# Per-token scalars of a four-layer graph network: products with ones against transfers through DRAM

## The chip, the cores and the metric

The kernel runs on one core of one Trainium2 chip. The metric is the device time of one execution in microseconds. A core has TensorE (PE, matmuls; its weight loads are shown apart as PEld), VectorE (DVE), ScalarE (ACT), GpSimd (POOL) and SyncE (SP), which here only issues transfers. ScalarE issues transfers too. Every engine has an instruction queue of its own; engines wait for one another by semaphores.

## The reference

128 graphs of 64 nodes, 512 features, all float32. `x` is [128, 64, 512], `adj` is [128, 64, 64], the node mask is one everywhere. Each of four layers is `x = x + f(relu(layernorm(x)), adj)`:

```python
def layer0(h, adj):            # q, k, v without bias
    agg = einsum('bij,bjd->bid', adj, k * mask)
    w   = inv_scale * mask * einsum('bid,bid->bi', q, agg)   # one scalar per token
    return softmax(w, axis=1)[:, :, None] * v                # over the 64 tokens of a graph
def layer1(h, adj):            # q, k, v with bias
    weight = adj * exp(einsum('bqd,bkd->bqk', q, k)); weight /= weight.sum(2)
    return einsum('bqk,bkd->bqd', weight, v)
def layer2(h, adj):            # 8 heads, output product with bias
    attn = softmax(scores * SCALE * (adj + adj)); return ctx @ Wo + bo
def layer3(X, A):
    Xw = X @ Wv + bv
    sj, si = Xw @ aw[:d], Xw @ aw[d:]                        # two scalars per token
    alpha = A * exp(leaky_relu(sj[:, None, :] + si[:, :, None] + ab, 0.2))
    t  = alpha / (alpha.sum(-1) + 1e-12)
    return relu(sum over k of (t^k X) @ Wk[k] + bk[k])
```

Layer 0 needs, for every token, the `w` of all 64 tokens of its graph. Layer 3 needs, for every token, the `si` of all 64 tokens of its graph.

## The kernel before

The 8192 tokens are worked in 32 blocks of 256 (TT = 2 halves of 128 partitions, so a half holds two graphs of 64). A block's 256x512 by 512x512 products are made in Strassen's manner: seven products instead of eight, with sums of the operands made on GpSimd (`sums`, L270 to L274) and sums of weights (`sums_of_weights`), which GpSimd forms while the kernel runs. `later` puts them on a list and `chore` (L100) takes some off it, each placed behind an instruction of GpSimd.

One `Product` (L278) holds two PSUM tiles, `ab` and `dc`, from four slots. `first` makes two of the seven products, `second` two, `late` three; between them `keep_ab` (L335 on ScalarE, L336 on VectorE) and `keep_dc` (L344) take partial results out of PSUM, and `store` (L358 to L362) makes the four quarters of the result on ScalarE, VectorE and GpSimd. A slot can be used again when its last reader is done. `side_by_side` runs two Products and calls the functions of a list `between` in three places: slot 0 behind the first Product's `first`, slot 1 ahead of the first `late`, slot 2 ahead of the second.

`norm` (L180) makes the layernorm of a block: statistics on VectorE (L185 to L189), `rstd` and `nmr` on GpSimd (L191, L193), `h` on ScalarE (L200), which also sends `h` to DRAM (`h_rows`, L204). SP reads it back in another arrangement (`part`, L217), and VectorE turns that into `hT` (L243), the stationary side of the products.

Layers 0 and 1 are interleaved in cycles of four steps (two blocks of layer 0, two of layer 1). Layer 2 runs over the 32 blocks, then layer 3. In layer 3, a step makes y2 and y1 side by side, then y0; two sums over neighbours stand between (`po2` ahead of y0's `late`, `po3` in the next step, L449). `layer3_end` takes po3 out by ScalarE (`tz`, L1013), adds y0 on GpSimd (L1015), and adds into `x` on VectorE (L1016). In the same step the norm of block b+2 runs and, at its end, `layer3_dots` (L915) makes that block's scalars `sij`.

A scalar of each token is put before all tokens of its graph in this way: VectorE multiplies `eye` (a 64x64 unit matrix in both halves of the partitions) with the scalars (`wd` L616, `di` L920), and TensorE multiplies by a matrix of ones for each graph:

```python
    def graph_sums(e, cols: int, name: str):
        ps = ps_sc.tile([P, cols], FP, tag="sc", name=f"sm_{name}")
        nc.tensor.matmul(ps, ones_bd, e, start=True, stop=True)
```

In layer 0, `layer0_end` reads that from PSUM (L627 to L643); in layer 3, `layer3_in` does (L934).

The tile scheduler of the language puts the instructions of each engine in one order ahead of time, by its own costs. `tc.issue_after(i)` makes it place what follows behind the instruction `i` on that order; in this way the source moves work. `tail[0]`, `kept_ab[0]`, `read[0]`, `taken` and `stored` are such instructions: the last of a layer's tail, the last `keep_ab`, the last issued read of `part` or `pT`, and the last readers in a `store`.

The seams are the steps where one layer's loop gives over to the next. At the seam to layer 2, `fetch2` loads x and `adj`, and `prepare2` adds a bias and makes the norm. At the seam to layer 3, `fetch3`, `layer3_norm` and `layer3_dots` of the first blocks are called in the last rounds of layer 2, and `biases3` (L889 to L894) loads three rows of `bk` spread over the partitions and adds them on GpSimd.

Of the kernel before, what the change touches and what calls it, by code (L numbers as in the profile page):

```python
# [13 lines left out]
P = 128  # L14
# [12 lines left out]
def kernel(ctx: ExitStack, tc: tile.TileContext, a: dict, out: bass.AP):  # L27
# [72 lines left out]
    def chore(n: int = 1):  # L100
        with tc.issue_after(behind[0].ins):
            for _ in range(min(n, len(chores))):
                w, (to, x, y) = chores.pop(0)
                nc.gpsimd.tensor_tensor(w[:, to], w[:, x], w[:, y], ALU.subtract)
# [63 lines left out]
    eye = const.tile([P, N], FP, tag="eye", name="eye")  # L168
    for g in range(2):
        h = slice(g * N, (g + 1) * N)  # L170
        nc.vector.memset(ones_bd[h, h], 1.0)
        nc.vector.tensor_copy(eye[h, :], ident[h, h])
# [4 lines left out]
    behind_norm, parted = {}, {}  # L177
    read, w2 = [None], []

    def norm(x, name: str, home):  # L180
# [13 lines left out]
        behind_norm.setdefault(0, (by_rows, summed_up))  # L194
        h = med.tile([P, TT, D], FP, tag="h", name=f"h_{name}", bufs=homes["h"])
# [60 lines left out]
    behind = [None]  # L256
# [21 lines left out]
    class Product:  # L278
# [77 lines left out]
        def store(self, y):  # L356

            nc.scalar.copy(y[:, 0, :F], self.a)  # L358
            nc.vector.tensor_tensor(self.u3, self.b, self.p1, ALU.add)
            nc.vector.tensor_tensor(y[:, 1, :F], self.d, self.u3, ALU.add)  # L360
            nc.vector.tensor_tensor(y[:, 0, F:], self.c, self.u2, ALU.add)
            nc.gpsimd.tensor_tensor(y[:, 1, F:], self.u3, self.p5, ALU.add)  # L362
# [91 lines left out]
    def graph_sums(e, cols: int, name: str):  # L454

        ps = ps_sc.tile([P, cols], FP, tag="sc", name=f"sm_{name}")
        nc.tensor.matmul(ps, ones_bd, e, start=True, stop=True)
        return ps

    def reciprocals(e, name: str):  # L460

        den = graph_sums(e.rearrange("p t i -> p (t i)"), TT * N, name)
        r = small.tile([P, TT, N], FP, tag="r", name=f"r_{name}", bufs=2)
        nc.vector.reciprocal(r.rearrange("p t i -> p (t i)"), den)
        return r
# [130 lines left out]
    def layer0(b: int, x, adjT, hs, hT, aggs, between):  # L596
# [11 lines left out]
        for t in range(TT):  # L608
            nc.vector.scalar_tensor_tensor(
                aggs[t], gv[:, 0, t, :], msc[:, b * TT + t : b * TT + t + 1], aggs[t],  # L610
                ALU.mult, ALU.mult, accum_out=w[:, t : t + 1],
            )


        wd = small.tile([P, TT, N], FP, tag="e", name=f"wd_{b}")
        tail[0] = nc.vector.tensor_tensor(  # L616
            wd,
            eye.unsqueeze(1).to_broadcast([P, TT, N]),
            w.unsqueeze(2).to_broadcast([P, TT, N]),
            ALU.mult,  # L620
        )
        return x, gv, w, wd

    def layer0_end(b: int, x, gv, w, wd):
        wrow = graph_sums(wd.rearrange("p t i -> p (t i)"), TT * N, f"w_{b}")
        mn = small.tile([P, TT], FP, tag="mx0", name=f"mn0_{b}")
        nc.vector.tensor_reduce(  # L627
            mn, wrow.rearrange("p (t i) -> p t i", t=TT), AX.X, ALU.min
        )
        nc.vector.tensor_tensor(w, w, mn, ALU.subtract)  # L630
        tot = small.tile([P, TT], FP, tag="tot", name=f"tot_{b}")
        for t in range(TT):
            nc.scalar.activation(
                wd[:, t, :], wrow[:, t * N : (t + 1) * N], AF.Exp, bias=mn[:, t : t + 1],
# [272 lines left out]
    def layer3_dots(b: int, x, adjT, hs):  # L907
# [4 lines left out]
        for s in range(2):  # L912
            for t in range(TT):
                hu = med.tile([P, D], FP, tag="agg", name=f"hu_{b}_{s}_{t}", bufs=2)
                nc.vector.scalar_tensor_tensor(  # L915
                    hu, hs[t], 1.0, us[s], ALU.mult, ALU.mult,
                    accum_out=sij[:, s, t : t + 1],
                )
        di = small.tile([P, TT, N], FP, tag="e", name=f"di_{b}")
        nc.vector.tensor_tensor(  # L920
            di,
            eye.unsqueeze(1).to_broadcast([P, TT, N]),
            sij[:, 1, :].unsqueeze(2).to_broadcast([P, TT, N]),
            ALU.mult,
        )
# [4 lines left out]
    def layer3_in(b: int, x, adjT, hs, e, sj, made: dict):  # L930


        pi = graph_sums(e.rearrange("p t i -> p (t i)"), TT * N, f"i_{b}")
        nc.vector.tensor_tensor(  # L934
            e,
            pi.rearrange("p (t i) -> p t i", t=TT),
# [188 lines left out]
    for i, (layer, b) in enumerate(steps):  # L1125
        if i == n_steps - 4:
            fetch2(0)
        if i == n_steps - 3:
            fetch2(1)
        if i == n_steps - 1:  # L1130
            fetch2(2)
        between = [[], [lambda: chore(3 if i < 4 else 1)], []]
# [20 lines left out]
        elif i + 2 == n_steps:  # L1153
            between[0].append(lambda: prepare2(0))
        else:
            between[0].append(lambda: prepare2(1))
        if layer == 0:
            softmax = layer0(b, *loaded[b], *normed[i], aggs.pop(b, None), between)
            begun = [(0, lambda b=b, softmax=softmax: layer0_end(b, *softmax))]
# [23 lines left out]
    def layer3_step(b: int, ahead: bool = True):  # L1183
# [8 lines left out]
        def begin():  # L1192
# [3 lines left out]
            if b + 2 < n_blk and ahead:  # L1196
                with tc.issue_after(kept_ab[0].ins):
# [16 lines left out]
        if b + 2 < n_blk:  # L1214
            with tc.issue_after(kept.ins):
                if ahead:
                    normed3 = layer3_dots(b + 2, *normed3)
                    fetch3(b + 3)
                else:
                    fetch3(b + 2)  # L1220
# [17 lines left out]
    for b in range(n_blk):  # L1238
        x = loaded2[b][0]
        first_in = lambda: layer3_in(0, *normed3, made_in) if b == n_blk - 2 else None  # L1240
        if b + 1 < n_blk:
            pTs = []
# [5 lines left out]
            def ahead():  # L1248
                with ExitStack() as placed:
                    for i in (pTs[1], kept_c[0], read[0]):  # L1250
                        placed.enter_context(tc.issue_after(i.ins))
                    prepare2(b + 3)
                with tc.issue_after(read[0].ins):
# [5 lines left out]
        else:  # L1259
            pTs = layer2_turned(b, es)  # L1260
# [6 lines left out]
        if b == n_blk - 2:  # L1267
            w3[0] = fetched("L3_Wk0", 4, nc.sync)
            later(w3[0])
            bias3 = biases3()  # L1270
        if b + 1 < n_blk:
            coming = values(b + 1, ops)
            next(coming)
        else:
# [15 lines left out]
        if b + 1 < n_blk:  # L1290
            with tc.issue_after(of_o.kept.ins):
                layer2_divided(b + 1, es)
        chore(2 if b == n_blk - 2 else 0)
# [3 lines left out]
        if n_blk - 3 <= b < n_blk - 1:  # L1297
            fetch3(b - n_blk + 3)
            normed3 = layer3_norm(b - n_blk + 3)
            with tc.issue_after(of_o.taken.ins):  # L1300
                normed3 = layer3_dots(b - n_blk + 3, *normed3)
        elif b == n_blk - 1:
            with tc.issue_after(of_o.taken.ins):
                normed3 = layer3_dots(2, *normed3)
            fetch3(3)
# [69 lines left out]
```

## Time and profile before

| | |
|---|---|
| time, median of 3 runs | 2525.49 us (2525.25 to 2526.71) |
| profiled execution | 2527.11 us, of which the span of instructions is 2524.5 us |
| mean granted clock of TensorE | 0.996 |
| TensorE matmul, busy | 2487.0 us, 19488 instructions |
| VectorE, busy | 1822.0 us, 4590 instructions |
| GpSimd, busy | 1324.1 us, 1710 instructions |
| ScalarE, busy | 857.1 us, 2106 instructions |
| transfers | 295.50 MB, 117 GB/s on average |

The profile comes from one execution. Its rows name an engine, a line of the kernel, an operation, the tiles that it writes and reads, and times. A wait is put down to the instruction or transfer that released it last. The clock is the share of TensorE's full speed that was granted in a stretch.

### The profile page before, as it was taken

Reading aid. Unit: us, or ns where it says so; the run is one execution under the profiler, and the core shown is the slowest. Engines: PE = TensorE matmul, PEld = TensorE weight load, DVE = VectorE, ACT = ScalarE, POOL = GpSimd, SP = SyncE. Lnnn points to the kernel's source line nnn. Section 1 sums busy time; section 2 is a strip of 40 time slices with the busy share of each in tenths; the row PEclk is TensorE's granted clock in tenths of the full one; section 3 lists DMA queues with packets and bytes.
Section 4 is the critical chain, followed back from the end, with each engine's and each line's share of the span. In section 5 each row is a group of like instructions: output and inputs, shape, how many; then the busy total and the mean of one; then the engine's idle time right before and its main releaser. Section 6 shows DMA issues by size and latency. Waiting matters only on the chain.

```text
span 2524.5 us, 52284 instructions
## 1 busy us (share of the span) xinstructions
PE 2487.0 (99%) x19488; PEld 2124.1 (84%) x19488; DVE 1822.0 (72%) x4590; ACT 857.1 (34%) x2106; POOL 1324.1 (52%) x1710
## 2 busy tenths in 40 slices
PE   9899999999999999999999999999989999999999
PEld 5788888888888888999999999999867777777776
DVE  5577777777777786667667667667568777777775
ACT  3333433333334332333333333333223333333332
POOL 2444343444433445666656556556465555555554
PEclk9999999999999999999999999999999999999999
DMA  7344343333343354443343343344433333333320
GB/s 180 94 127 124 111 127 114 119 107 116 113 126 112 122 156 138 128 133 108 122 132 115 123 131 115 122 136 134 139 112 104 104 103 107 105 106 106 103 77 34
DMA packets 305190, 295.50 MB, mean 117 GB/s; under 512 B 56870, under 2 KB 211494, under 8 KB 304936
## 3 DMA queue, kind: packets, MB, share of 16 engines
q1 hardware_dynamic: 258856, 208.26, 29.2%
q10 hardware_dynamic: 46080, 83.91, 9.1%
q8 instruction: 153, 2.51, 0.4%
q14 instruction: 101, 0.83, 0.1%
HBM read 158.91 MB, written 133.18 MB: 116 GB/s over the span
## 4 chain that ended last, share of the span: by engine, by line
PE 57%; DVE 2%; DMA 1%; POOL 1%; issue 1%; SPq 0%; ACT 0%; POOLq 0%; ACTq 0%; DVEq 0%
PE ab_y L306 13%; PE dc_y L306 9%; PE ab_v L306 4%; PE ab_q L299 4%; PE ab_k L299 4%; PE ab_o L306 4%; PE dc_q L299 3%; PE dc_k L299 3%; PE dc_v L306 3%; PE dc_o L306 3%; PE po L449 2%; PE pc L825 1%; PE s L750 1%; DVE hu L915 1%; DMA x<-x 0%
## 5 line engine op out<-in xcount | busy, mean ns | idle before, releaser
L200 ACT ACTIVATE h<-x,nmr,rstd 128x512 f32<-128x512 f32 x256 | 194.8, 806 | 207.6 <-POOL nmr L193 202.1
L270 POOL TENSOR_TENSOR S<-hT 128x256 f32<-128x256 f32 x128 | 97.8, 764 | 243.9 <-DVE hT L243 231.1
L306 PE MATMUL ab_y<-L_Wk,hT 128*128 128x256 f32 x768 | 204.9, 389 | 7.9 <-DVE u_y L336 6.7
L306 PE MATMUL ab_v<-L_Wv,hT 128*128 128x256 f32 x768 | 201.0, 384 | 3.7 <-DVE u_v L336 3.0
L306 PEld LDWEIGHTS ab_y<-L_Wk,hT 128*128 128x128 f32 x768 | 138.7, 190 | 74.9 <-DVE u_y L336 30.7
L191 POOL TENSOR_TENSOR rstd<-ve,neghalf 128x2 f32<-128x2 f32 x128 | 90.5, 707 | 209.2 <-DVE mv L189 190.7
L306 PE MATMUL dc_v<-L_Wv,S 128*128 128x256 f32 x768 | 198.0, 380 | 0.7 <-ACT p_v L344 0.7
L306 PE MATMUL ab_y<-L_Wk,S 128*128 128x256 f32 x768 | 198.0, 380 | 0.0
L306 PE MATMUL ab_v<-L_Wv,S 128*128 128x256 f32 x768 | 197.1, 379 | 0.0
L306 PE MATMUL dc_y<-L_Wk,S 128*128 128x256 f32 x768 | 193.5, 380 | 0.1
L243 DVE STREAM_TRANSPOSE hT<-part 128x512 f32<-128x512 f32 x252 | 174.4, 698 | 8.6 <-DMA part<-h_rows 5.9
L306 PEld LDWEIGHTS dc_y<-L_Wk,S 128*128 128x128 f32 x768 | 146.0, 191 | 21.3 <-issue 0.8
L306 PEld LDWEIGHTS ab_y<-L_Wk,S 128*128 128x128 f32 x768 | 146.5, 191 | 20.1
L185 DVE BATCH_NORM_STATS2 stats<-x 128x6 f32<-128x512 f32 x256 | 162.8, 677 | 0.0
L306 PEld LDWEIGHTS ab_v<-L_Wv,S 128*128 128x128 f32 x768 | 145.9, 190 | 19.8
L306 PEld LDWEIGHTS dc_v<-L_Wv,S 128*128 128x128 f32 x768 | 143.8, 191 | 20.0 <-ACT p_v L344 0.9
L306 PEld LDWEIGHTS ab_v<-L_Wv,hT 128*128 128x128 f32 x768 | 138.2, 190 | 21.9 <-DVE u_v L336 4.0
L915 DVE SCALAR_TENSOR_TENSOR hu<-h,us 128x512 f32<-128x512 f32 x128 | 139.4, 1139 | 1.9 <-POOL bs L894 1.4
L1015 POOL TENSOR_TENSOR tz<-tz,y 128x512 f32<-128x512 f32 x62 | 90.4, 1458 | 95.4 <-ACT tz L1013 95.3
L336 DVE TENSOR_TENSOR u_v<-ab_v,p_v 128x256 f32<-128x256 f32 x96 | 40.4, 421 | 126.4 <-ACT p_v L335 125.9
L1016 DVE SCALAR_TENSOR_TENSOR x<-tz,x 128x512 f32<-128x512 f32 x62 | 42.9, 692 | 112.3 <-POOL tz L1015 112.3
L272 POOL TENSOR_TENSOR S<-hT,S 128x256 f32<-128x256 f32 x128 | 113.0, 883 | 0.0
(257 smaller groups left out, 6181.7 us busy)
## 6 DMA issues: line engine op xcount, KB each, us to landing
x<-x SPq DMA_DIRECT2D x128, 512.0 KB, 3.8
h_rows<-h ACTq DMA_DIRECT2D x252, 256.0 KB, 2.1
part<-h_rows SPq DMA_DIRECT2D x504, 128.0 KB, 2.8
x<-in_x_dram SPq DMA_DIRECT2D x32, 512.0 KB, 3.7
e_rows<-et ACTq DMA_DIRECT2D x64, 256.0 KB, 3.0
pT<-e_rows SPq DMA_DIRECT2D x128, 128.0 KB, 3.1
out_dram<-x SPq DMA_DIRECT2D x31, 512.0 KB, 2.8
adjT<-in_adjT_dram SPq DMA_DIRECT2D x64, 64.0 KB, 2.2
```

What stands on the lines that cost most here:

```text
L185: nc.vector.bn_stats(stats[:, t, :], x[:, t, :])
L191: nc.gpsimd.tensor_tensor(rstd, ve, neghalf, ALU.pow)
L200: nc.scalar.activation(hs[t], x[:, t, :], AF.Relu, bias=nmr[:, t : t + 1], scale=rstd[:, t : t + 1])
L243: nc.vector.transpose(hT[:, :, t * P : (t + 1) * P].rearrange("p k (g q) -> p g k q", q=Q), part[:, t * 4 : (t + 1) * 4].rearrange("p g (k ...
L270: nc.gpsimd.tensor_tensor(S1, A21, A22, ALU.add)
L272: nc.gpsimd.tensor_tensor(S4, A12, S2, ALU.subtract)
L299: nc.tensor.matmul(dst[:, m * P : (m + 1) * P], w[:, place, k, m * P : (m + 1) * P], left[:, k, :], start=key not in self.begun, stop=last ...
L306: nc.tensor.matmul(dst, left[:, k, :], w[:, place, k, :], start=key not in self.begun, stop=last and k == 1, skip_group_check=True,)
L449: nc.tensor.matmul(ps[t][half[g ^ t]], e[half[g], t, :], us[t][half[g]], start=True, stop=True)
L915: nc.vector.scalar_tensor_tensor(hu, hs[t], 1.0, us[s], ALU.mult, ALU.mult, accum_out=sij[:, s, t : t + 1],)
L1015: nc.gpsimd.tensor_tensor(tz[t], tz[t], y0[:, t, :], ALU.add)
L1016: nc.vector.scalar_tensor_tensor(x[:, t, :], tz[t], 0.0, x[:, t, :], ALU.max, ALU.add)
```

## The change

Five things are changed together.

1. `spread` takes the place of `graph_sums` and of the products with `eye`, in layer 0 (for `w`) and layer 3 (for `si`): SP writes the 256 scalars of a block as rows into DRAM, and reads them back twice, once for each 64 partitions, repeated over the partitions. The result lies in SBUF instead of PSUM, and `layer3_in` and `layer0_end` work in its place.
2. `layer0_end` is called in slot 1 of the next step instead of slot 0, and `tail` is the last of layer 0's dots.
3. `chore`'s weight sums are placed also behind the last `store` on GpSimd and the last `nmr`.
4. At the seam from layer 1 to 2, `fetch2` comes earlier and the norm of block 0 and 1 is placed behind `tail`. At the seam from layer 2 to 3, the loads, norms and dots of blocks 0 and 1 come earlier and are placed by hand, the last block's turning of `e` comes earlier, and the loads of the biases come behind the reads of `pT`.
5. In layer 3, the norm of block b+2 is placed behind `spread_out` (the last read of the spread) as well as behind `kept_ab`, and the load of block b+3 behind the reads of `part`.

```diff
+    spread_out = [None]
+
+    def spread(of_tokens, name: str):
+        row = tc.dram_tile([TT, P], FP, name=f"{name}_row")
+        nc.sync.dma_start(row.rearrange("t p -> p t"), of_tokens)
+        to = small.tile([P, TT, N], FP, tag="e", name=name)
+        by_graph = row.rearrange("(o t) (g i) -> g o t i", o=1, g=2)
+        for g in range(2):
+            spread_out[0] = nc.sync.dma_start(
+                to[half[g]], by_graph[g].to_broadcast([N, TT, N])
+            )
+        return to
...
-    def chore(n: int = 1):
-        with tc.issue_after(behind[0].ins):
+    def chore(n: int = 1, also=()):
+        with ExitStack() as placed:
+            for i in (behind[0], *also):
+                placed.enter_context(tc.issue_after(i.ins))
...
+        normalised[0] = by_rows
...
+            stored[0] = nc.gpsimd.tensor_tensor(y[:, 1, F:], self.u3, self.p5, ALU.add)
...
-        wd = small.tile([P, TT, N], FP, tag="e", name=f"wd_{b}")
-        tail[0] = nc.vector.tensor_tensor(
-            wd, eye..., w..., ALU.mult)
-        return x, gv, w, wd
+        return x, gv, w, spread(w, f"w_of_{b}")
...
-        wrow = graph_sums(wd.rearrange("p t i -> p (t i)"), TT * N, f"w_{b}")
...
+        nc.vector.tensor_reduce(mn, wd, AX.X, ALU.min)
...
-        di = small.tile([P, TT, N], FP, tag="e", name=f"di_{b}")
-        nc.vector.tensor_tensor(
-            di, eye..., sij[:, 1, :]..., ALU.mult)
+        di = spread(sij[:, 1, :], f"si_of_{b}")
...
-        pi = graph_sums(e.rearrange("p t i -> p (t i)"), TT * N, f"i_{b}")
...
-        if i == n_steps - 4:
-            fetch2(0)
-        if i == n_steps - 3:
-            fetch2(1)
-        if i == n_steps - 1:
-            fetch2(2)
-        between = [[], [lambda: chore(3 if i < 4 else 1)], []]
+        if i >= n_steps - 6 and i % 2 == 0:
+            fetch2((i + 6 - n_steps) // 2)
+        between = [[], [
+            lambda: chore(3 if i < 4 else 1, (stored[0], normalised[0]) if i else ())
+        ], []]
...
-            begun = [(0, lambda b=b, softmax=softmax: layer0_end(b, *softmax))]
+            begun = [(1, lambda b=b, softmax=softmax: layer0_end(b, *softmax))]
...
             if b + 2 < n_blk and ahead:
-                with tc.issue_after(kept_ab[0].ins):
+                with tc.issue_after(kept_ab[0].ins), tc.issue_after(spread_out[0].ins):
                     normed3 = layer3_norm(b + 2)
...
                 if ahead:
                     normed3 = layer3_dots(b + 2, *normed3)
-                    fetch3(b + 3)
+                    with tc.issue_after(read[0].ins):
+                        fetch3(b + 3)
...
-            pTs = layer2_turned(b, es)
...
-            bias3 = biases3()
...
+            if b == n_blk - 2:
+                normed3 = layer3_dots(
+                    1, *normed3_1[0], (of_qk[b + 1][1].taken, kept_ab[0])
+                )
...
+        if b == n_blk - 2:
+            with tc.issue_after(read[0].ins):
+                fetch3(2)
+                fetch3(3)
+            with tc.issue_after(of_o.taken.ins):
+                pTs = layer2_turned(b + 1, es)
+            with tc.issue_after(read[0].ins):
+                bias3 = biases3()
...
-        if n_blk - 3 <= b < n_blk - 1:
-            fetch3(b - n_blk + 3)
-            normed3 = layer3_norm(b - n_blk + 3)
+        if b == n_blk - 3:
+            fetch3(0)
+            fetch3(1)
+            with tc.issue_after(read[0].ins):
+                normed3 = layer3_norm(0)
             with tc.issue_after(of_o.taken.ins):
-                normed3 = layer3_dots(b - n_blk + 3, *normed3)
+                normed3 = layer3_dots(0, *normed3)
```

## The prediction

> **What bounds the kernel now.** I read the page's busy times first, then TensorE's waits and three stretches, then the order of one step of layer 3.
>
> ```profile
> PE 2487.0 (99%) x19488; PEld 2124.1 (84%) x19488; DVE 1822.0 (72%) x4590; ACT 857.1 (34%) x2106; POOL 1324.1 (52%) x1710
> ...
> PE 57%; DVE 2%; DMA 1%; POOL 1%; issue 1%; SPq 0%; ACT 0%; POOLq 0%; ACTq 0%; DVEq 0%
> ```
>
> TensorE is busy for 2487.0 of 2524.5 us, so at most 37.5 us of idle time can be had by moving work, plus whatever products are removed. VectorE has 28% to spare as an average, which says little about one step.
>
> ```profile
> PE ab_y L306 <- DVE u_y L336: 6.7, 2, 6.5
> ...
> PE sm_w L457 <- DVE wd L616: 4.5, 2, 3.9
> PE ab_g L306 <- DVE u_g L336: 3.9, 2, 3.2
> ...
> PE pc L825 <- DMA pT<-e_rows: 2.8, 2, 1.7
> ```
>
> These are TensorE's waits (total, times, longest). The 6.5 and the 2.8 lie at the seam from layer 2 to 3, the 3.9 and the 3.2 in the first 100 us. By stretches:
>
> ```profile
> 300.00:900.00 600.00, 599.76 (x4227) 514.26 (x4226) 446.44 (x1206) 231.90 (x600) 242.19 (x365) 1.00 0.39 118
> 960.00:1740.00 780.00, 780.00 (x8510) 719.02 (x8507) 540.98 (x1265) 255.41 (x661) 474.49 (x604) 1.00 0.41 124
> 1900.00:2470.00 570.00, 570.00 (x2999) 451.83 (x2998) 448.68 (x1141) 183.50 (x383) 332.70 (x381) 1.00 0.32 101
> ```
>
> The columns after the length are busy TensorE, weight loads, VectorE, ScalarE, GpSimd, then the granted clock. In all three steady stretches TensorE never waits at full clock. A removed product there is time saved, and a new wait there is time lost, undiluted.
>
> **Products removed.** TensorE at the sum of one block of layer 3:
>
> ```profile
> 2110.51 0.38 PE L457 MATMUL sm_i<-di,ones_bd 128*128 128x128 f32 x2
> 2110.73 1.03 PE L306 MATMUL ab_y<-L_Wk,hT 128*128 128x256 f32 x4
> ```
>
> From start to start it takes 0.22 us; in layer 0 (718.98 to 719.20) the same. 64 of them: 14.1 us at most. The 64 VectorE products with `eye` (0.28 us each, 18 us) go too, but VectorE isn't what ends the steps above.
>
> **What stands in their place.** A row write of 256 four-byte elements, then two reads that wait for it, all on SP: 192 issues more (0.33 to 0.46 us each, so about 1.2 us a block on a queue that is mostly idle). No transfer like it is in the trace. The nearest rows:
>
> ```profile
> adjT<-in_adjT_dram SPq DMA_DIRECT2D x64, 64.0 KB, 2.2
> ...
> c_row<-c SPq DMA_DIRECT2D x4, 0.5 KB, 6.3
> ```
>
> The reads should land like `adjT` (2.2). The write lies between 2.2 and 6.3; `c_row` also moves four-byte elements, but stood beside 256 KB broadcasts at the start, so I take about 2.5. With two issues the chain is about 5.5 us, at most 9.3. The Trainium skill ("DMA: Bandwidth & Descriptors", Anatomy of one DMA) gives a DMA a fixed cost of about 2.0 us, spent mostly on the receipt of the last byte, which speaks against two dependent transfers in place of a product; by it the chain would be an estimated 4.9 us, and the 6.3 of `c_row` says that it can be much more.
>
> **Layer 3, 28 steady steps of 20.9 us.** The decisive edit is not the transfer but what is tied to it: `layer3_norm(b+2)` is now issued behind `spread_out`, so its BN statistics (VectorE L185) come after the four `hu` products instead of before `y<-po`. One step before:
>
> ```profile
> 2116.47 1.28 DVE L185 BATCH_NORM_STATS2 stats<-x 128x6 f32<-128x512 f32 x2
> ...
> 2123.06 0.90 DVE L915 SCALAR_TENSOR_TENSOR hu<-h,us 128x512 f32<-128x512 f32 x1
> ...
> 2132.74 0.69 DVE L1016 SCALAR_TENSOR_TENSOR x<-tz,x 128x512 f32<-128x512 f32 x1 [1.16 <-POOL tz L1015]
> 2133.35 0.42 DVE L359 TENSOR_TENSOR u_y<-ab_y,p_y 128x256 f32<-128x256 f32 x1
> ```
>
> ScalarE's `h` of the same block stood at 2119.34, where ScalarE had 1.9 us to spare; in the new order it stands, with its two DMA issues, directly ahead of the last `p_y` and of `tz` (L1013). So `tz` queues behind `h`, `h` behind GpSimd's `rstd`, that behind VectorE's statistics, those behind `hu`. I count from the first half of po2 (2117.6 on this step's clock):
>
> - `y<-po` 2.27, then two `hT` and four `y0` operations 2.53 (2120.53 to 2123.06): 4.8.
> - four `hu` 4.24 (to 2127.30): 9.05. `sj` 0.13, statistics 1.2: 10.4. Aggregates, `ve`, `mv` and one `u_y`: 11.2.
> - `rstd` and `nmr` (2118.32 to 2119.30) 0.98: 12.2. Two `h` and their issues (2119.34 to 2121.21) 1.9: 14.1. `p_y`: 14.45, where `tz` starts. Before it started at 2128.82, that is 11.2: 3.2 us later.
> - `tz` to GpSimd 0.77, GpSimd 1.26, `x` 0.65, `u_y` of y2 (L359, L360 in the changed file) 0.42: 17.55. TensorE wants that PSUM slot for y0 at 2134.22 less the 0.22 removed, 16.4: it waits 1.1. The second `tz` on GpSimd ends at 18.3, `x` at 18.95, the two `y` that free the other slot at 19.65, and y0's second half starts at about 19.85 where it was at 18.35 (2135.95).
>
> So a step grows by about 1.5 with the removed product already counted. Each hand-over is uncertain by some 0.1, and GpSimd and VectorE will overlap a little differently; I take 1.4 x 28 = +39. From below: the chain hides wholly and only 0.22 a step is saved, -6. From above: the write takes 6.3, `si_of` lands at about 9.05 + 0.4 + 6.3 + 0.5 + 2.2 = 18.45, and its addition, which VectorE has ahead of both `x`, moves `y` from 19.65 to 21.35: 1.7 x 28 = 48 more. At my 5.5 it lands at 14.6, before `x` at 16.5, free. On SP the two reads wait for the write, and behind them stand the reads of `part`, which wait for `h` at 14 anyway: no loss.
>
> That `fetch3(b+3)` moves behind the reads of `part` costs nothing: x is asked for at about 19 and used in the next step at 31.
>
> **Layers 0 and 1, 15 cycles of four steps.** Their spreads have a whole slot to land, and what is queued behind them on SP (loads of x and `part`) is asked for more than a step ahead: hidden at 5.5 us, and up to the +15 below if not. Each cycle loses two sums (0.44). With `layer0_end` in slot 1, its reduction, exponentials and `x` additions (1.34 to 1.84 us on VectorE) now stand ahead of the `gT` stores, and the norm of the pair that follows stands on ScalarE ahead of `p_v`. By hand `p_v` comes within 0.3 us of its need, and the `gT` slot 0.2 to 0.7 late. A cycle nets -0.44 to +1.0; I take +0.2: +3 (from -6 to +15).
>
> **Start.** The 3.9 at `sm_w` came from the dots waiting for GpSimd's y (L362) behind weight sums; `chore` now stands behind `stored`. The 3.2 at `ab_g` followed from the same queue. Both went with about 2 us of slowed products. Up to -9; but layer 0's first spreads meet the weight loads that made `c_row` 6.3, and VectorE's `mn0` stands in order: up to +5. I take -4.
>
> **Seam 1 to 2.** Earlier loads of layer 2: TensorE idles 3.2 us in 940 to 960. -2 (0 to -3).
>
> **Seam 2 to 3.** TensorE idles 2.8, 6.5 and 1.5 here.
>
> ```profile
> 1800.00:1830.00 30.00, 27.24 (x291) 25.36 (x290) 20.34 (x46) 7.69 (x22) 14.58 (x17) 0.94 0.60 157
> 1830.00:1850.00 20.00, 13.49 (x53) 11.05 (x53) 11.35 (x24) 1.76 (x5) 17.59 (x19) 0.83 0.34 109
> ```
>
> The 6.5 was `u_y` L336 behind `hu` L915 behind GpSimd's `bs` L894; `dots(1)` is now earlier and the biases are behind pT's reads. The three groups after it took 4.88 us where 2.6 is usual, so the clock adds 2.3. Up to -13; the new waits (si_of(0) ahead of `qk`'s VectorE work, another load in the way) take 0.3 to 5 back. -10.
>
> **Sum:** 39 + 3 - 4 - 2 - 10 = +26 on the profiled execution, 2527.1 (span 2524.5 and 2.6 around it): 2553; the median lies 1.6 lower, so 2551. A measurement of this kernel tells about 0.2%, 5 us, from no change.
>
> **Rivals.**
> A. Layer 3 keeps TensorE as its bound (faster). The place is the same chain; it decides at a `tz` less than about 2.3 us late instead of 3.2, since the other terms give 13 and 13 over 28 steps is 0.46 a step, 0.9 less than I read. If it hides wholly: -6 + 3 - 4 - 2 - 10 = -19, 2506; with layers 0 and 1 and the seams at their best, 2490. For it: ScalarE is 34% busy and the norm has a whole step to spare. Against: engines here keep their written order, and the order puts `h` ahead of `tz`.
> B. The row write is slow (near 6.3) also in layer 3. Then 2551 + 48 at the worst, near 2570 to 2600. For it: only one row of four-byte writes, and it says 6.3. Against: DMA share is 0.32 there and 0.59 at the start.
> C. The gains and the chain cancel (layer 3 at +0.3 to +0.6 a step): 2520 to 2530.
>
> **Chances.** Forecast (2535 to 2570) 0.52; A 0.28; B 0.13; C 0.07. Leaving out A's lowest and B's highest, the range is 2499 to 2578. Faster by over 0.2%: A and a part of C, 0.31; within: 0.04; slower: 0.65.
>
> **What would show it.** In the changed profile, layer 3's stretch should hold new TensorE waits on `ab_y` and `dc_y` released by VectorE's `u_y` L360 and `y`, about 1 us a step, and a period near 22.3; `tz` on ScalarE directly behind `h`. `si_of` should land within 6 us of its write's issue. The wait of 6.5 and the 3.9 should be gone. I am wrong if the period is 20.7, if `si_of` is what VectorE waits for, or if layers 0 and 1 grow by more than 15 us.

## The result, and the profile after

The changed kernel takes 3007.61 us (median of 4 runs, 2999.23 to 3009.02) against 2525.53 us: 1.190 times as long, interval 1.188 to 1.192. The forecast was slower, at 2551 us, with 2578 as the upper end: the sign was right and the size was off by a factor of nineteen. The profiled execution took 3008.35 us, its span is 3006.6 us, the mean granted clock 0.936. Of the 12 runs of l3_best below, two fell in a slower state (2576.39 and 5172.51 us), and its time is the median of the other ten.

The page of the changed kernel, its busy times and its chain:

```profile
PE 2618.2 (87%) x19360; PEld 2206.1 (73%) x19360; DVE 1786.6 (59%) x4524; ACT 855.8 (28%) x2106; POOL 1318.8 (44%) x1710
...
PE 54%; DMA 20%; DVE 16%; issue 3%; POOL 3%; ACT 2%; SPq 1%; ACTq 0%; DVEq 0%; POOLq 0%
```

Transfers are now 20% of the chain that ends last, where they were 1%. TensorE has 128 matmuls fewer and is busy 131 us *longer*; its idle time went from 37.5 to 388.4 us. Both add up to the 482 us of the span. Who is waited for, first on TensorE, then on VectorE:

```profile
PE ab_y L307 <- DVE u_y L360: 210.2, 30, 8.7
PE ab_v L307 <- DVE u_v L337: 74.4, 18, 6.7
```

```profile
DVE si_of L918 <- DMA si_of<-si_of_row: 317.8, 31, 12.0
DVE mn L619 <- DMA w_of<-w_of_row: 212.5, 32, 10.1
```

TensorE waits for VectorE's `u_y`, which does no more than before; VectorE waits 31 times for `si_of` and 32 times for `w_of`, each about 10 and 7 us. The transfers, in the list of DMA issues (the last number is the median time from issue to landing):

```profile
x<-x SPq DMA_DIRECT2D x128, 512.0 KB, 4.4
...
w_of<-w_of_row SPq DMA_DIRECT2D x64, 32.0 KB, 4.2
si_of<-si_of_row SPq DMA_DIRECT2D x64, 32.0 KB, 3.7
...
w_of_row<-w SPq DMA_DIRECT2D x32, 1.0 KB, 8.2
...
si_of_row<-sij SPq DMA_DIRECT2D x32, 1.0 KB, 9.0
```

The write of 1 KB takes about twice as long as the transfers of 512 KB (`x<-x`, 4.4 us). One step of layer 3, on SP, VectorE and TensorE:

```profile
2616.39 0.36 SPq L460 DMA_DIRECT2D si_of_row<-sij  x1
2626.22 1.23 SPq L464 DMA_DIRECT2D si_of<-si_of_row  x2
```

```profile
2629.81 0.29 DVE L918 TENSOR_TENSOR si_of<-si_of,sj 128x128 f32<-128x128 f32 x1 [11.04 <-DMA si_of<-si_of_row]
...
2630.95 0.42 DVE L360 TENSOR_TENSOR u_y<-ab_y,p_y 128x256 f32<-128x256 f32 x1
```

```profile
2600.08 2.07 PE L307 MATMUL ab_y<-L_Wk,hT 128*128 128x256 f32 x4 [7.15 <-DVE u_y L360]
...
2607.08 1.13 PE L307 MATMUL ab_y<-L_Wk,hT 128*128 128x256 f32 x4
...
2631.42 0.80 PE L307 MATMUL ab_y<-L_Wk,hT 128*128 128x256 f32 x1 [7.83 <-DVE u_y L360]
```

The write is issued at 2616.39, the reads can start only at 2626.22, `si_of` is added at 2629.81: 13.4 us. `u_y` stands behind that addition on VectorE, and TensorE's y0 behind `u_y`. In the kernel before, the same addition of block b+1 stood behind both `x` and behind y2's first stores, where it held up neither:

```profile
2134.54 0.28 DVE L934 TENSOR_TENSOR di<-sm_i,sj 128x128 f32<-128x128 f32 x1
```

So the change also brought the reader forward on VectorE. A step takes 31.3 us (2600.08 to 2631.42) where it took 20.9. After such a wait four matmuls take 2.07 us instead of 1.13: the granted clock is 0.50 from 2600.1 to 2604.0. Over layers 0 and 1 it is 0.93 on average and over layer 3 0.90, where it was 1.00 and 0.99; that is where most of the 131 us of busy time come from. The Trainium skill ("TensorE: Matmul & The Clock Gate", Part 1) says that an idle window of about 3.4 us puts TensorE back to half its clock; the 0.50 after a wait of 7.15 us agrees. A shorter wait can bring it here too: in l3_best_norm_late, below, four matmuls took 2.07 us after a wait of 1.86 us, at a granted clock of 0.50, while in pairs four took 1.13 us after a wait of 2.67 us. In the runs below whose waits in a step stay at or under 3.6 us (prod_norm_late, l3_best_norm_late, quick, pairs) busy time rises by 12 to 26 us instead of 131.

Where the time went, by stretches cut at TensorE's first product of layer 2, its last q product of layer 2, and its first product of layer 3 (profiled executions, us; "seam" is from the second cut to the third; the versions below are explained with their experiments):

| kernel | layers 0, 1 | layer 2 | seam | layer 3 to the end |
|---|---|---|---|---|
| before | 961.0 | 846.7 | 24.3 | 692.5 |
| changed | 1155.1 | 845.4 | 35.0 | 971.1 |
| pairs | 1007.0 | 845.6 | 28.0 | 790.4 |
| quick | 995.0 | 845.6 | 24.9 | 764.7 |
| late_in | 1167.5 | 845.4 | 31.5 | 802.2 |
| l3_best_norm_late | 961.2 | 845.7 | 29.7 | 769.4 |
| l3_best | 961.9 | 845.6 | 29.8 | 680.4 |
| prod | 965.5 | 845.8 | 22.3 | 683.4 |
| prod_slot1 | 959.6 | 845.9 | 22.3 | 683.5 |
| prod_seam | 957.3 | 845.9 | 22.7 | 683.8 |
| l0_quick | 994.4 | 845.8 | 22.4 | 683.4 |
| final | 955.8 | 845.6 | 20.9 | 678.1 |

### The profile page after: what moved, and what is told of

Same layout as the page of the kernel before. It is cut to its first block, busy times and chain, and to the rows that moved or that the text cites. A ratio compares the mean times of both kernels' runs of the same rounds, so it can differ in the third digit from the quotient of the medians.

```text
span 3006.6 us, 52286 instructions
## 1 busy us (share of the span) xinstructions
PE 2618.2 (87%) x19360; PEld 2206.1 (73%) x19360; DVE 1786.6 (59%) x4524; ACT 855.8 (28%) x2106; POOL 1318.8 (44%) x1710
## 4 chain that ended last, share of the span: by engine, by line
PE 54%; DMA 20%; DVE 16%; issue 3%; POOL 3%; ACT 2%; SPq 1%; ACTq 0%; DVEq 0%; POOLq 0%
PE ab_v L307 9%; DMA si_of_row<-sij 8%; PE dc_v L307 6%; DVE hu L906 4%; PE ab_y L307 4%; PE ab_q L300 4%; PE ab_k L300 4%; DMA w_of<-w_of_row 4%; PE ab_o L307 4%; DMA si_of<-si_of_row 4%; DMA w_of_row<-w 3%; PE dc_q L300 3%; PE dc_k L300 3%; PE dc_o L307 3%; PE dc_y L307 2%
## 5 line engine op out<-in xcount | busy, mean ns | idle before, releaser
L307 PE MATMUL ab_y<-L_Wk,hT 128*128 128x256 f32 x768 | 234.9, 434 | 220.8 <-DVE u_y L360 210.2
L307 PEld LDWEIGHTS ab_y<-L_Wk,hT 128*128 128x128 f32 x768 | 153.2, 211 | 303.7 <-DVE u_y L360 222.2
L307 PE MATMUL ab_v<-L_Wv,hT 128*128 128x256 f32 x768 | 217.8, 409 | 85.3 <-DVE u_v L337 74.4
L307 PE MATMUL ab_y<-L_Wk,S 128*128 128x256 f32 x768 | 223.6, 419 | 0.0
L307 PE MATMUL ab_v<-L_Wv,S 128*128 128x256 f32 x768 | 209.5, 398 | 0.0
L918 DVE TENSOR_TENSOR si_of<-si_of,sj 128x128 f32<-128x128 f32 x32 | 10.0, 314 | 317.8 <-DMA si_of<-si_of_row 317.8
L307 PEld LDWEIGHTS ab_y<-L_Wk,S 128*128 128x128 f32 x768 | 163.9, 213 | 27.1
L307 PEld LDWEIGHTS dc_y<-L_Wk,S 128*128 128x128 f32 x768 | 156.9, 205 | 33.2 <-ACT p_y L345 5.4
L336 ACT COPY p_y<-ab_y 128x256 f32<-128x256 f32 x96 | 35.7, 372 | 385.2 <-PE ab_y L307 384.7
L363 POOL TENSOR_TENSOR y<-u_y,p_y 128x256 f32<-128x256 f32 x64 | 57.2, 894 | 188.1 <-DVE u_y L360 188.1
L619 DVE TENSOR_REDUCE mn<-w_of 128x2 f32<-128x128 f32 x32 | 9.2, 286 | 212.5 <-DMA w_of<-w_of_row 212.5
```

Of the source, the lines that this page charges most:

```text
L307: nc.tensor.matmul(dst, left[:, k, :], w[:, place, k, :], start=key not in self.begun, stop=last and k == 1, skip_group_check=True,)
L336: kept_p[0] = nc.scalar.copy(self.p1, self.a)
L363: stored[0] = nc.gpsimd.tensor_tensor(y[:, 1, F:], self.u3, self.p5, ALU.add)
L619: nc.vector.tensor_reduce(mn, wd, AX.X, ALU.min)
L918: nc.vector.tensor_tensor(e, e, sj.unsqueeze(2).to_broadcast([P, TT, N]), ALU.add,)
```

## The experiments

**Theory.** What costs is the length of the spread, most of it the write, because VectorE's order puts its reader ahead of work that TensorE waits for. Rivals: the order of the norm (the prediction's own mechanism), the number of transfers on SP, the other edits.

**Why the write is slow: probe.** Writes that nobody reads, in seven forms, added to the kernel before.

```diff
+        nc.sync.dma_start(to, of)    # form = b % 7, behind layer3_dots
```

> The kernel before, with one more transfer a block of layer 3 that nobody reads: the write of the scalars to DRAM in seven forms in turn (block number modulo 7), on SP behind the same dots. fa4: the change's own form, 256 elements of four bytes to one run of 1 KB. fb8: the same bytes as 128 pieces of 8. fc64 and fd512: 256 elements of four bytes, each 64 or 512 bytes from the next. fe_half: 128 elements of four bytes. ff_quarter: 64 elements. fg_wide: 128 pieces of 256 bytes. Theory (each small piece costs the queue by itself): fa4, fc64 and fd512 all land in 8 to 9 us as in the changed kernel, fb8 and fe_half in about 5, ff_quarter in 3 to 4, fg_wide near 5 or less. Rival (neighbouring elements fall into the same short stretch of DRAM and their writes wait for one another): fc64 and fd512 land in about 2.5 us, fa4 in 8 to 9. Second rival (it is the traffic around it): all seven land alike, in 2 to 4 us here. The time stays at 2525 to 2530 in all cases, since nobody waits.

```profile
fg_wide<-h SPq DMA_DIRECT2D x4, 32.0 KB, 1.8
...
fa<-sij SPq DMA_DIRECT2D x5, 1.0 KB, 9.5
fb<-sij SPq DMA_DIRECT2D x5, 1.0 KB, 3.6
fc<-sij SPq DMA_DIRECT2D x5, 1.0 KB, 1.7
fd<-sij SPq DMA_DIRECT2D x5, 1.0 KB, 1.7
fe_half<-sij SPq DMA_DIRECT2D x4, 0.5 KB, 8.6
ff_quarter<-sij SPq DMA_DIRECT2D x4, 0.2 KB, 6.6
```

The theory of a price for each piece fell: the same 256 pieces of four bytes land in 1.7 us when they lie 64 bytes apart, and in 9.5 side by side. That rules out the traffic around as well. The run took 2531.0 us, 1 us more than expected.

**How near is too near: probe2 and probe3.**

```diff
+            to = tc.dram_tile([TT, P, pitch], FP, ...)[:, :, 0]   # pitch 2, 4, 8: px, py, pz
+            to = tc.dram_tile([16, P], FP, ...)[:, :8]            # qf: runs of 8, 512 bytes apart
+            to = tc.dram_tile([8, 16], FP, ...).rearrange("a e -> e a")   # qg: turned
```

> The kernel before, again with transfers in layer 3 that nobody uses, block number modulo 8. px, py, pz: the 256 four-byte scalars written with 8, 16 and 32 bytes from one to the next (contiguous they landed in 9.5 us, 64 bytes apart in 1.7). pw: 32 of them, contiguous. ra, rb, rc: what reads them back over 64 partitions, from a contiguous row (the change's read), from pairs of 8 bytes side by side, and from a row spaced by 64 bytes. Theory (writes into the same 64 bytes of DRAM wait for one another): the time falls with the number that share them, px about 5, py about 3, pz about 2, pw about 5. Rival (they wait only where they touch the next one): px, py and pz all about 1.7. Reads: ra 2.5 to 4, rb no longer than ra, rc far longer (10 us or more), since it moves 16384 pieces of four bytes.

> The kernel before with unread writes of four-byte scalars in layer 3, one column, block number modulo 7. qa: 32 contiguous, qb: 64 contiguous, qd: 128 contiguous (8.6 before). qc: 16 pairs of 8 bytes, contiguous. qe: 128 spaced by 8 bytes. qf: 16 runs of 8 neighbours, the runs 512 bytes apart, so that pieces of the same run come from neighbouring partitions. qg: 128 contiguous in DRAM but turned, so that neighbours in DRAM come from partitions 8 apart and neighbouring partitions lie 64 bytes apart. Theory A (pieces that follow one another on one DMA engine wait where they touch the same 64 bytes; neighbouring partitions go to the same engine): qf about as long as qd, qg about 2 us. Theory B (pieces of different engines collide in the same 64 bytes): qf 4 us or less, qg about as long as qd.

```profile
px<-sij SPq DMA_DIRECT2D x4, 1.0 KB, 4.3
py<-sij SPq DMA_DIRECT2D x4, 1.0 KB, 2.7
pz<-sij SPq DMA_DIRECT2D x4, 1.0 KB, 1.9
...
pw<-sij SPq DMA_DIRECT2D x4, 0.1 KB, 1.3
```

```profile
qa<-sij SPq DMA_DIRECT2D x5, 0.1 KB, 4.1
...
qd<-sij SPq DMA_DIRECT2D x5, 0.5 KB, 7.1
...
qf<-sij SPq DMA_DIRECT2D x4, 0.5 KB, 1.8
qg<-sij SPq DMA_DIRECT2D x4, 0.5 KB, 7.3
```

At 4, 8, 16, 32 and 64 bytes from piece to piece the write takes 9.5, 4.3, 2.7, 1.9 and 1.7 us. So it is closeness in DRAM that costs, and pieces need not touch for it. Runs of eight touching pieces from neighbouring partitions are quick (`qf` 1.8) if the runs lie 512 bytes apart. 128 touching pieces are slow also when neighbours in DRAM come from partitions 8 apart (`qg` 7.3), so it is not that neighbouring partitions touch: theory A is out. Theory B fits both, but it is not the only reading, since the time also rises with the number of touching pieces: `pw`, from 16 partitions, takes only 1.3, well under what was expected, 32 pieces take 4.1 (`qa`), 128 take 7.1 (`qd`). A run of eight pieces from far partitions was not written, so whether the far partitions or the long run is what counts stays open, as does the unit in DRAM. A slow write can also hold up what follows it: `rowb` of probe2, in the form of `fb` and issued 0.5 us behind a row in the change's form, landed in 8.5 us, where `fb` took 3.6.

Of the reads, the change's own took 3.4, from pairs 3.0, from a row spaced by 64 bytes 6.7 each for four reads instead of two, less than the 10 that were expected. The runs took 2526.1 and 2529.2 us.

**The write alone: pairs, and later quick.** The changed kernel with a different row in DRAM.

```diff
-        row = tc.dram_tile([TT, P], FP, name=f"{name}_row")
-        nc.sync.dma_start(row.rearrange("t p -> p t"), of_tokens)
+        row = tc.dram_tile([P, TT], FP, ...)       # pairs: 8 bytes a partition
+        row = tc.dram_tile([16, P], FP, ...)[:, :8 * TT]   # quick: 16 runs of 64 bytes, 512 apart
```

> The changed kernel with one edit: the row in DRAM holds the two scalars of a partition side by side (128 pieces of 8 bytes, 3.6 us in the probe instead of 9.5), and each partition reads 512 bytes in one piece. Nothing is moved. Theory (the length of the spread is what VectorE waits for, step by step): some 5.5 us less a block in layer 3 and about as much in layer 0, so 2660 to 2740. Rival (the number of transfers on SP costs as well): over 2800.

> The changed kernel with the quick row in both layers and nothing else altered: the write lands in about 2 us where it took 9, the spread in about 6.5 where it took 13. Theory (the write is most of it, the rest is the late norm and the remaining wait in both layers): layer 2 starts at 990 to 1000, layer 3 takes 750 to 780, total 2600 to 2630. If the order alone costs what l3_best_norm_late showed and the quick spread is hidden: 2570 to 2590. Rival (the transfers' number): 2660 or more, as with pairs.

2672.8 and 2632.1 us. The writes landed in 3.0 to 3.5 us with pairs and 1.8 to 2.3 with quick, and 335 and 376 of the 482 us went, with no instruction moved. TensorE's busy time fell from 2618.2 to 2512.8 and 2503.4, with the shorter waits. Quick missed its expected range by 2 us.

**The reader moved: late_in.** The spread as it was, its reader in layer 3 behind y0's stores.

```diff
-            if b + 1 < n_blk:
+            if b + 1 < n_blk and not b:
                 layer3_in(b + 1, *coming, made_in)
...
+        if b and b + 1 < n_blk:
+            with tc.issue_after(kept.ins):
+                layer3_in(b + 1, *coming, made_in)
```

> The changed kernel with the spread in both layers as it is, but layer3_in of block b+1 behind y0's last store in step b instead of ahead of both x additions: VectorE comes to si_of about 16 us later in the step. Theory (the chain of some 13 us only costs because VectorE's order has its reader in front of work that TensorE waits for): layer 3 falls from 971 to 690 to 735 us, the total to 2725 to 2770, layers 0 and 1 unchanged. Rival (the transfers themselves slow others, by the queue on SP or the DMA engines): layer 3 stays above 850 us.

2848.4 us; layer 3 fell from 971.1 to 802.2, so the reader's place is most of what layer 3 lost. That lies between the two expectations (690 to 735, and above 850), and layers 0 and 1, which this does not touch, took 12 us more. What was undercounted is above all the late norm, as the next runs show. With it and no wait for a spread layer 3 takes 769.4 (l3_best_norm_late); what the other 33 us are was not traced.

**The norm: prod_norm_late, prod, and l3_best_norm_late.** Products back in both layers; then the norm in its old place; and the same pair with the spread.

```diff
-        di = spread(sij[:, 1, :], f"si_of_{b}")
+        di = beside_eye(sij[:, 1, :], f"di_{b}")    # both kernels; w in layer 0 likewise
...
+        pi = graph_sums(e, f"i_{b}")
...
-                with tc.issue_after(kept_ab[0].ins), tc.issue_after(spread_out[0].ins):
+                with tc.issue_after(kept_ab[0].ins):
                     normed3 = layer3_norm(b + 2)
...
-                    with tc.issue_after(read[0].ins):
-                        fetch3(b + 3)
+                    fetch3(b + 3)
```

> The changed kernel with the products with ones back in both layers (layer0_end again in slot 0), but with all other edits, and the norm of layer 3 as late in VectorE's order as in the changed kernel. Theory (the spread's length is what costs): nearly all of the 482 us go, but the late norm keeps the chain from hu through the statistics, rstd, h and tz, so layer 3 runs at 22.3 us a step: 2535 to 2555. Rival (the order of the norm costs nothing by itself): 2508 to 2516. Rival (the other edits, weight sums and seams, cost a large part): over 2600.

> The same, with the norm of layer 3 back in its old place (its two conditions and the one on fetch3 taken off). What is left of the change is the order of the weight sums and both seams. Theory: layer 3 at 20.9 us a step, the start and the seams better by what the prediction gave them, -16: 2508 to 2516. Rival (the edits at the seams give nothing): 2523 to 2530.

2595.48 us (1.0284, 1.0268 to 1.0299) and 2515.99 us (0.9967, 0.9956 to 0.9979). The late norm costs 79.5 us over 28 steps, 2.8 a step. That is more than was expected of the late norm (2555 at most) and less than of a large cost of the other edits (over 2600). Part of it there is the products' own: TensorE waits 40.9 us for a slot of PSUM that `tz` still reads. So the pair was repeated with the spread, whose reader comes a whole step later and never waits:

```diff
-                layer3_in(b + 1, *coming, made_in)
+            with tc.issue_after(kept_ab[0].ins):
+                layer3_in(b, *held3.pop(b), made_in)    # held3[b]: what layer3_dots(b) left
...
-        first_in = lambda: layer3_in(0, *normed3, made_in) if b == n_blk - 2 else None
+        first_in = lambda: held3.update({0: normed3}) if b == n_blk - 2 else None   # l3_best
```

> The version with products (2516) with the spread in layer 3 alone, in the change's slow form, but layer3_in of block b one step later, in step b itself behind y1's keep_ab: the transfer has more than 20 us, and VectorE's order is that of the kernel before. Theory (the transfer costs nothing where its reader comes later than it lands, and a product is worth 0.22 us): 2516 less 31 times 0.22, 2507 to 2511. Rival (192 small transfers disturb TensorE's supply in other ways): 2520 or more.

> l3_placed with block 0 of layer 3 treated like the others: its layer3_in no longer stands in layer 2's last rounds, where VectorE waited 9.4 us for its spread ahead of qk, but in step 0. Spread in layer 3 in the change's slow form, products in layer 0, norm in its old place. Theory: the 9.4 go, and the 0.22 of each block of layer 3 is left as a gain over the version with products (2516): 2508 to 2513. Rival (the transfers cost elsewhere): 2516 or more.

> l3_best with the norm of layer 3 as late as in the change (both its conditions, and fetch3 behind the reads). No reader waits for a spread, and no product takes a slot of PSUM: this is the prediction's chain from hu to tz alone. As predicted, 1.4 to 1.5 us a step: 39 to 42 us slower than l3_best. If the 2.8 us a step that the late norm cost in the version with products hold here too: 75 to 80. If the chain has slack: 0 to 10.

l3_placed: 2524.97 us (0.9999, 0.9989 to 1.0009), a miss. Layer 3 is at 681.2 us there, but one wait at the seam is left:

```profile
PE ab_v L307 <- DVE qk L376: 9.4, 1, 9.4
```

It is block 0's spread, whose reader stands in layer 2's last rounds ahead of `qk`, as in the change (9.5 there). l3_best takes it away: 2519.66 (0.9977, 0.9967 to 0.9986), above what was expected, since the seam still takes 29.8 us where prod has 22.3; the quick row of best_quick brings it to 21.7 (1803.8 to 1825.5), so there too it is the write's length. In l3_best layer 3 takes 680.4 us, 3 less than with products (prod 683.4): the slow transfers by themselves cost next to nothing in it. With the late norm 2609.59 (two runs): 90 us more than l3_best, 3.2 a step, above all three expectations. One step of it, on VectorE, and GpSimd's store beside the second `x`:

```profile
2211.58 0.69 DVE L1020 SCALAR_TENSOR_TENSOR x<-tz,x 128x512 f32<-128x512 f32 x1 [4.43 <-POOL tz L1019]
2212.19 0.42 DVE L360 TENSOR_TENSOR u_y<-ab_y,p_y 128x256 f32<-128x256 f32 x1
2213.43 1.20 DVE L1020 SCALAR_TENSOR_TENSOR x<-tz,x 128x512 f32<-128x512 f32 x1 [0.82 <-POOL tz L1019]
...
2218.51 2.28 DVE L981 SCALAR_TENSOR_TENSOR y<-po,r,y 128x512 f32<-128x512 f32 x3 [0.49 <-PE po L450]
```

```profile
2213.36 0.73 POOL L363 TENSOR_TENSOR y<-u_y,p_y 128x256 f32<-128x256 f32 x1
```

The next `y<-po` starts at 2218.51, and the `hT` that follows comes 23.5 us after that of the step before (2197.36 to 2220.83). Quick, the changed kernel with nothing but the quick row, takes 764.7 in layer 3, no more than these 769.4. So the two mechanisms account for layer 3: with the write quick, what is left of its loss is no more than the late norm costs.

**Layer 0: l0_placed, prod_slot1, l0_quick.** The spread in layer 0 alone, with `layer0_end` a step later; its place in slot 1 without a spread; its place with a quick spread.

```diff
-            begun = [(0, lambda b=b, softmax=softmax: layer0_end(b, *softmax))]
+            begun = [(1, lambda b=b, softmax=softmax: layer0_end(b, *softmax))]   # prod_slot1, l0_quick
+            after_next.append(lambda b=b, softmax=softmax: layer0_end(b, *softmax))   # l0_placed
```

> The version with products (2516) with the spread in layer 0 alone, in the change's slow form, and layer0_end not in the next step but in the one after it, behind the tail of the step between. Theory: the wait at w_of goes, and 31 products less: 2507 to 2513. Rival (the x additions and exponentials so placed delay the stores of the step they fall into): 2520 to 2560. If the spread's wait stays on VectorE: over 2600.

> The version with products (2516) with layer0_end in slot 1 of the next step, as in the change. Theory (the place alone costs little, the spread's length costs the rest): 2516 to 2522. Rival (the x additions ahead of the gT stores are what costs): 2530 to 2600.

> The version with products in layer 3, and in layer 0 the change's spread and its layer0_end in slot 1, but with a row in DRAM made of 16 runs of 64 bytes, the runs 512 bytes apart, each from 8 neighbouring partitions (such runs of 32 bytes landed in 1.8 us in the probe), so the spread takes about 6 us in place of 13. Theory: the first product of layer 2 starts at 960 to 1000 us where it started at 1155 in the changed kernel, total 2515 to 2555. Rival (it is the number of transfers, or the order): over 2580.

2552.46 us (1.0098, 1.008 to 1.0117; in the rival's range), 2513.52 us (0.9952, 0.9934 to 0.997) and 2547.8 us. The place in slot 1 costs nothing, it rather gains. A spread of some 6 us there still costs 35 us up to layer 2 (994.4 against 959.6), so layer 0's reader comes sooner than the transfer's end even then (VectorE waits 40.6 us for `w_of` in l0_quick). With the reader a step later VectorE waits only 4.1 us for `w_of` in all, but TensorE waits for `u_v` and `u_g` (18.0 and 12.1 us in l0_placed); what holds these up I did not trace. Neither version with a spread in layer 0 alone paid; the quick row with the reader a step later was not run.

**What is left: l3_best_seam, prod_seam, best_quick, final.** l3_best and prod with the seam from layer 1 to 2 as before; the first of these with the quick row of above (best_quick); that with `layer0_end` in slot 1 (final).

```diff
-        if i >= n_steps - 6 and i % 2 == 0:
-            fetch2((i + 6 - n_steps) // 2)
+        if i == n_steps - 4:
+            fetch2(0)
+        ...
```

> The same, with the seam from layer 1 to 2 as before (fetch2 later, the norms of blocks 0 and 1 not behind the tail). Theory (that edit gains nothing: TensorE idles 5.0 us in 900 to 1000 us with it and 3.2 without): 2 to 5 us faster than the one above. Rival (it gains the 2 us that the prediction gave it): 2 us slower.

> The version with products (2516) with the seam from layer 1 to 2 as in the kernel before: what is left of the change is the order of the weight sums and the seam to layer 3. Theory (the first seam's edit loses some 3 us, as l3_best and l3_best_seam showed): 2511 to 2515. Rival: 2516 or more.

> l3_best_seam (2517) with the quick row for layer 3's spread. Theory (its 6 us of idle TensorE at the seam to layer 3 are waits for the slow write and what queues behind it on SP): 2509 to 2514. Rival (the transfers' place, not their length, disturbs that seam): 2515 to 2518.

> best_quick (2505.6) with layer0_end in slot 1 of the next step, which gained 2.5 us in the version with products. If the gains add: 2502 to 2504. If not: 2505 to 2508.

2516.95 us (0.9963, 0.9951 to 0.9974), 2512.65 (0.9948, 0.9936 to 0.9961), 2505.56 (0.9921, 0.9907 to 0.9934; better than the 2509 to 2514 expected) and 2502.03 us (0.9910, 0.9893 to 0.9926). The last beats both kernels: products in layer 0, a quick spread read a step later in layer 3, the norm where it was, the weight sums and the seam to layer 3 as the change has them. Its page:

```profile
PE 2474.1 (99%) x19424; PEld 2113.3 (85%) x19424; DVE 1812.5 (72%) x4558; ACT 861.4 (34%) x2106; POOL 1309.3 (52%) x1710
```

## Why the prediction was right or wrong

- **The reading of the profile held.** In the steady stretches a removed product is time saved undiluted: best_quick is 7.1 us faster than prod_seam, 31 or 32 products at 0.22 as read off 2110.51 and 2110.73. And new waits there were time lost undiluted.
- **The step that failed is the price of the row write.** The term that was mis-sized is the chain of about 5.5 us for a spread, which took 13.4. For the write I had one row of its kind, `c_row` at 6.3 us, and 2.2 for reads; I took 2.5, on the ground that `c_row` stood beside large loads. That ground was never tested, and the probe shows it false: the same form takes 9.5 us in layer 3, where the traffic is light (DMA share 0.32 before). Even the upper end was too low: `si_of` was to land at worst at 18.45 us after po2, and was added 22.6 us after the start of `y<-po` (2607.18 to 2629.81). "The decisive edit is not the transfer but what is tied to it" is so the wrong way round: the quick row alone takes 206 us out of layer 3 and 160 out of layers 0 and 1, and the late norm costs 77 to 90. Rival B had the right mechanism, at 13%, with too small a price. That the sign was right is not luck, since the late norm alone makes the kernel slower; but it says little, as most of the loss came from elsewhere.
- **The place of the reader was half seen.** I wrote that the addition stands ahead of both `x` on VectorE and counted 1.7 us a step for a late landing. Measured, a step grew by 10.4 us. With the quick row layer 3 falls by 206 us of its 279, with the reader moved (late_in) by 169; the two overlap, since each takes away the same wait.
- **The clock was left out.** I counted it at the seam (2.3 us) and not in a steady step. But waits like that of 7.15 us come in nearly every step (210.2 us in 30), and the clock falls after them; TensorE's busy time grew by 131 us, about half of it in layer 3 and half in layers 0 and 1.
- **The late norm: right mechanism, half the size.** The chain was right to 0.1 us as far as `u_y`: in l3_best_norm_late `tz` starts 14.46 us after `y<-po` (counted 14.45), `u_y` ends after 17.56 (17.55). But I set the start 0.6 us after po2's first matmul, where VectorE starts 1.1 after it, and the second `x` took 1.20 us beside GpSimd's store, not 0.69. Most steps take 23.5 us, 2.6 more than before, not 1.4; the average is 3.2 us more than l3_best, since some steps take over 25 us, as where the clock falls after the wait of 1.86 us. Whether `fetch3` behind the reads costs nothing, as I wrote, no run shows by itself: each run that put the norm back took that condition off with it. In l3_best_norm_late, which has it, VectorE waits for no load of x in layer 3.
- **Layers 0 and 1** were the worst term in proportion: +3, at most +15, measured +194 up to layer 2's first product, start and first seam included. I wrote that the spreads have a whole slot to land. VectorE waited 6.6 us a block for them (212.5 over 32), and with the quick row of some 6 us still 40.2 us in all. Behind the spreads on SP stand the reads of `part`, for which VectorE waits 29.0 us in the changed kernel and 5.9 before, most of it here (26.0). The cost of the order, which I counted by hand, was the smaller matter: prod_slot1 has it and takes 2513.52 us, prod 2515.99 (medians of different sets).
- **The start** was right in size: prod_seam, which has only the order of the weight sums there, reaches layer 2 at 957.3 instead of 961.0, -3.7 where -4 was taken (one profile each). Of its mechanism half came true: the 3.9 at `sm_w` is gone, but the wait at `ab_g` that was to go with it is still there, 4.1 us where it was 3.2.
- **Seam 1 to 2** was wrong in sign: l3_best is 2.7 us slower with that edit than l3_best_seam, and prod 3.3 slower than prod_seam (medians of different sets), where -2 was taken; a new wait of 3.8 us at `den` goes with it.
- **Seam 2 to 3** was right for the edit (-11.1 from seam and layer 3 in prod, -10 taken) and wrong for the change: the wait for `si_of(0)` ahead of `qk` that I priced at 0.3 to 5 is 9.5.

## What to carry to other kernels

When an operation has one row of its kind in the trace, that row is its price until something shows otherwise; to explain it away by its surroundings is a guess, and the forecast has to be worked out at the high price before it is set aside. A product of 0.22 us may be replaced by a chain of transfers, at a gain, but only where the reader is a whole step away in its engine's order, and in layer 0 not even then (l0_placed); so first look for how late the reader can stand. And a wait that comes in every step must be counted with the slow matmuls that follow it.

## What the runs showed of the hardware

A DMA that writes 256 scalars of four bytes from 128 partitions side by side into 1 KB of DRAM lands in 8.2 to 9.5 us; 64 bytes apart they land in 1.7, and as 16 runs of 64 bytes, 512 bytes apart, in 1.8 to 2.3. A small transfer can so be slower than one of 512 KB (4.4 us). The Trainium skill ("DMA: Bandwidth & Descriptors", Specifications) says that below 512 bytes a transfer does read-modify-write; the runs agree that small writes can be slow, but show that closeness in DRAM decides, since the spaced ones are as small. Its fixed cost of about 2.0 us for a transfer, which the prediction drew on and which the page gives for transfers issued from GpSimd, is about met by the spaced writes from SP (1.7) and missed more than fourfold by those side by side. On VectorE, the same addition `x` of 128x512 in l3_best_norm_late took 1.20 us in the 28 cases in which GpSimd's `y` addition (L363) had begun before it, and 0.68 to 0.69 us in the other 36, also where an addition on GpSimd began during it.
